# A 64-row pair in place of two 128-row matmuls for the sums that a recurrence adds to later nodes

## The chip, the cores and the metric

The kernel runs on one core of one Trainium2 chip. The metric is the device time of one launch, in microseconds (us): the median over several runs. A profile is one further execution, recorded by the hardware profiler. Five engines matter here: TensorE (PE in the profile; its weight loads are listed apart as PEld), VectorE (DVE), ScalarE (ACT), GpSimd (POOL) and SyncE (SP), which issues most DMAs.

## The reference

Four graph layers follow one another on 16 graphs (B = 16) of 1024 nodes (N) with 256 features (D), all in float32. Each layer is `x = x + layer(relu(layernorm(x)))`, with one adjacency matrix per graph. Layers 0, 1 and 3 are sums over neighbours and dense products. Layer 2, which the change is in, is a recurrence over the nodes:

```
def step(h, i):                                  # for every node i, in order
    x_par = adjT_normalised[:, i] @ h            # sum over the neighbours, by their newest state
    r, z  = sigmoid(split(x[i] @ W_ioux.T + b + x_par @ W_iouh.T + b))
    hc    = tanh(x[i] @ W_coux.T + b + (x_par * r) @ W_couh.T + b)
    h[i]  = z * x_par + (1 - z) * hc
```

Node i needs the new states of earlier nodes and the old states of later ones. The adjacency has about 3% of its entries set.

## The kernel before

**Blocks and sub-blocks.** Layer 2 (`layer_2`, L542) takes the nodes in NT = 8 blocks of P = 128, and each block in NS = 8 sub-blocks of S = 16 nodes. Inside a block the nodes are put in an order of their own, made earlier, so that few nodes of a sub-block depend on each other. The 16 graphs are taken together: a tile holds G2 = 2 groups of GB = 8 graphs, and the 128 partitions of a group are 8 graphs x 16 nodes, the graph the slower index. So the state `h` of a sub-block is [128 rows (graph, node), 2 groups, 256 features].

**One sub-block** is K rounds (`round_`, L807; K is 1 for sub-blocks 0 to 4, then 2, 2 and 4; KS) and, where the graphs call for it, more rounds under a condition. A round is 8 matmuls into `pr` and 8 into `pz`, sigmoids on ACT, products on DVE, 8 matmuls into `pc`, a tanh on ACT, and per group two DVE instructions that give the new `h` (L844, L845). Between two rounds stands `change` (L792).

**What a finished sub-block owes to later nodes** is h times adjacency. `Sub.behind` (L703) spreads the adjacency rows into `bd`, [128 rows (graph, node), group, 8 graphs, later nodes]: row (graph b, node i) is zero in the columns of every graph but b. Three kinds of matmuls use it: `near` (L990) for the next 16 nodes, `next_block` (L750, L752) for the first 16 nodes of the next block, and `far_tasks` (L756) for the rest of the block. The rest is far = 96, 80, 64, 48, 32 or 16 nodes after sub-blocks 0 to 5, and none later. For each of 2 groups, 2 halves c of the features and 2 halves of the 8 graphs there is one far task: one matmul with 4 x far columns (L765) into a PSUM tile `pf`, and one DVE addition into `bxt`, the running sums of the block (L768).

**Fillers.** Far tasks are not run where they arise. They go as `behind` into the list `todo` of the following sub-block, mixed evenly (L918 to L920) with `share`: the tasks of `base_tasks` (L576), which build the next block's first sums from the other seven blocks. BASES says how many graphs are taken in a sub-block (1, 1, 2, 2, 2, 2, 2, 4); for each graph there are 7 matmuls of 256 columns (L616), all into one `pf` tile that is held until ACT has read it (L603), and one turning step (L630) into a `pf` tile of its own. In block 7 there is no next block and no share.

`fill(weight)` (L924) issues the first part of the list at the beginning of the sub-block and the rest in steps. With K = 1 there are two steps: a part of 0.357 ahead of the round's matmuls, and all the rest behind the `pc` matmuls. The parts are measured by each task's own cost, 0.0067 * far for a far task. What must be done behind a task's matmul (the addition, the copy) goes into `late` and is issued by `evict` (L788): in `round_` once behind the `pz` matmuls, and once behind the DVE instructions that give the new `h`.

**Order and buffers.** PE, DVE, ACT and POOL run their instructions in the order in which the program issues them (`manual_schedule`, L869). PSUM has 8 banks: `pr`, `pz`, `pc`, `pnx` and one `pa` take five, and `pf` has the other three (`bufs=3`). Far tasks, base tasks, turning steps and the input products of the next sub-block (`Gates`, L737 and L729) all take their tiles from these three. A fourth tile is written when the first one's reader is through.

Of the kernel before, what the change touches and what calls it, by code (L numbers as in the profile page):

```python
# [9 lines left out]
F32 = mybir.dt.float32  # L10
# [6 lines left out]
P = 128  # L17
B, N, D, H = 16, 1024, 256, 1024
NT = N // P
DC = D // P  # L20
HC = H // P
S = 16
NS = P // S
G2 = 2
GB = B // G2
# [14 lines left out]
def gnn_stack(ctx: ExitStack, tc: tile.TileContext, a: dict, out: bass.AP):  # L40
    nc = tc.nc
# [500 lines left out]
    def layer_2(shared, early):  # L542
        with ExitStack() as st:
            wp = st.enter_context(tc.tile_pool(name="w2", bufs=1))
            psum = st.enter_context(tc.tile_pool(name="psum2", bufs=1, space=PSUM))
# [202 lines left out]
            def next_block(h, bd, n, start):  # L748

                for c in range(DC):  # L750
                    for g in range(G2):
                        nc.tensor.matmul(pnx[:, c, g * GR : (g + 1) * GR], h[:, g, c * P : (c + 1) * P],  # L752
                                         bd[:, g, :, n : n + S], start=start and c == 0 and g == 0, stop=True,
                                         skip_group_check=True)

            def far_tasks(bxt, h, sub):  # L756


                bd, s = sub.bd, sub.s
                far = P - (s + 2) * S  # L760

                def task(g, c, b4):
                    def run():
                        pf = psum.tile([P, 4, far], F32, name="pf", bufs=3)
                        nc.tensor.matmul(pf, h[:, g, c * P : (c + 1) * P], bd[:, g, b4 : b4 + 4, S : S + far],  # L765
                                         start=True, stop=True)
                        to = bxt[:, c, g * GB + b4 : g * GB + b4 + 4, P - far :]
                        return lambda: nc.vector.tensor_add(to, to, pf)  # L768
                    return 0.0067 * far, run
                tasks = []  # L770
                if far > 0:
                    tasks = [task(g, c, b4) for g in range(G2) for c in range(DC) for b4 in (0, 4)]
                if sub.n > P - s * S:
                    tasks.append((0.9, lambda: next_block(h, bd, P - (s + 1) * S, s == 0)))
                return tasks
# [7 lines left out]
            def add(to, lhsT, rhs):  # L783
                nc.tensor.matmul(to, lhsT, rhs, start=False, stop=True, skip_group_check=True)
# [84 lines left out]
            with tc.manual_schedule(engines={mybir.EngineType.PE, mybir.EngineType.DVE, mybir.EngineType.Activation, mybir.EngineType.Pool}):  # L869
# [3 lines left out]
                bxt = shared.tile([P, DC, B, P], F32, name="bxt")  # L873
# [13 lines left out]
                for t in range(NT):  # L887
# [10 lines left out]
                    for s in range(NS):  # L898
# [36 lines left out]
                        for c in range(DC):  # L935
                            to = x[:, c].rearrange("p (b i) -> p b i", b=B)
# [10 lines left out]
                        h = work.tile([P, G2, D], F32, name="h")  # L947
# [38 lines left out]
                        if s + 1 < NS:  # L986
                            near = psum.tile([P, DC, G2 * GR], F32, name="pa")
                            for c in range(DC):
                                for g in range(G2):
                                    nc.tensor.matmul(near[:, c, g * GR : (g + 1) * GR], h[:, g, c * P : (c + 1) * P],  # L990
                                                     sub.bd[:, g, :, :S], start=True, stop=True)
                            behind = far_tasks(bxt, h, sub)
                        elif t + 1 < NT:
                            next_block(h, sub.bd, 0, False)
                            near = pnx
                            behind = last_tasks(t + 1, bxt_next)
                            bxt, he = bxt_next, he_next
# [221 lines left out]
```

## Time and profile before

| | |
|---|---|
| median of 7 runs | 4944.09 us (4938.64 to 4954.79) |
| profiled execution, device time | 4950.51 us |
| its span, first to last instruction | 4948.8 us, granted TensorE clock 0.979 |
| PE busy | 4621.6 us (93%) |
| DVE busy | 2386.8 us (48%) |
| far matmuls (L765), two passes each | 768 passes, 220.7 us busy |
| far additions (L768) | 384, 209 to 555 ns each |

The recurrence lies between about 1450 and 3500 us of the span; far tasks run from 1589.5 to 3428.5 us. A float32 matmul appears in the profile as two passes, each with a weight load (PEld) of its own, so 384 far matmuls are 768 rows. "Mean ns of one" is from a pass's start to its modelled end, longer than the distance to the next pass, because passes overlap: the distance between starts is what a pass takes of PE. In the timeline a row's first two numbers are the start of a group of equal instructions and the time from there to the end of its last one.

### The profile page before, as it was taken

To read this page: it belongs to the slowest core of one execution; us is meant where nothing else is said; L and a number is where in the kernel's file an instruction comes from. 1 tells how busy PE (TensorE), PEld (TensorE's weight loads), DVE (VectorE), ACT (ScalarE), POOL (GpSimd) and SP (SyncE) were. 2 spreads that over 40 slices of the span, in tenths; PEclk is the share of its full clock that TensorE was granted. 3 is DMA by queue.
4 is the path that set the end of the run, shared out by engine and by line. 5 is a ranking of instruction groups with operands and counts; after the bars stand their busy time and mean duration, and the time that the engine had idled before them with its cause. 6 is when DMAs were issued, how large, how long until landed. Compare 5 with 4: busy or idle time off the path is not lost. (4 is left out here: it accounts for less than half of the span.)

```text
span 4948.8 us, 52564 instructions
## 1 busy us (share of the span) xinstructions
PE 4621.6 (93%) x18431; PEld 3061.8 (62%) x18431; DVE 2386.8 (48%) x6366; ACT 1174.6 (24%) x2388; POOL 1599.1 (32%) x1883
## 2 busy tenths in 40 slices
PE   8898899999997999999999999998799999999999
PEld 4443455565555777777777777776365555555656
DVE  6667754446443454445454545455534434334343
ACT  1111112112111222222222222222222323223232
POOL 3122333334323323233222222332523424234232
PEclk9999999999998999999999999999899999999999
DMA  4432335454536444544343434431422222222200
GB/s 157 120 94 94 95 94 179 165 170 151 181 118 191 130 143 121 162 140 149 116 143 106 152 121 158 128 127 34 149 85 85 77 77 85 77 95 69 83 26 17
DMA packets 530500, 577.13 MB, mean 117 GB/s; under 512 B 41552, under 2 KB 438992, under 8 KB 527824
## 3 DMA queue, kind: packets, MB, share of 16 engines
q1 hardware_dynamic: 499056, 460.79, 29.6%
q0 software_dynamic: 31040, 111.44, 6.4%
q8 instruction: 195, 3.19, 0.3%
q14 instruction: 209, 1.71, 0.1%
HBM read 470.17 MB, written 116.65 MB: 119 GB/s over the span
## 5 line engine op out<-in xcount | busy, mean ns | idle before, releaser
L290 PE MATMUL pa<-at,h 128*128 128x512 f32 x1088 | 489.3, 602 | 29.4 <-DVE ag L295 29.4
L1094 PE MATMUL ph<-ag,w 128*128 128x512 f32 x1024 | 479.4, 611 | 33.9 <-DVE hh L1098 33.8
L1132 PE MATMUL po<-w,hh 128*128 128x256 f32 x2048 | 447.7, 379 | 0.0
L616 PE MATMUL pf<-hb,ab 128*128 128x256 f32 x1568 | 422.6, 389 | 22.1 <-ACT bs L603 18.8
L1132 PEld LDWEIGHTS po<-w,hh 128*128 128x128 f32 x2048 | 387.8, 190 | 59.3 <-issue 7.9
L290 PE MATMUL pa<-at,q 128*128 128x512 f32 x960 | 420.8, 594 | 0.0
L290 PEld LDWEIGHTS pa<-at,h 128*128 128x128 f32 x1088 | 207.1, 193 | 269.5 <-issue 227.3
L1094 PEld LDWEIGHTS ph<-ag,w 128*128 128x128 f32 x1024 | 179.1, 190 | 295.9 <-DVE hh L1098 152.2
L1100 POOL TENSOR_TENSOR ss<-ss,sq 128x512 f32<-128x512 f32 x224 | 302.8, 1352 | 121.7 <-ACT sq L1097 117.4
L616 PEld LDWEIGHTS pf<-hb,ab 128*128 128x128 f32 x1568 | 286.4, 195 | 75.2 <-ACT bs L603 26.0
L983 POOL DMA_INDIRECT hs_d<-h,table x128 | 129.9, 1015 | 624.4 <-DVE gz L739 448.9
L290 PEld LDWEIGHTS pa<-at,q 128*128 128x128 f32 x960 | 179.5, 190 | 223.9 <-issue 220.9
L737 PE MATMUL pf<-wx,hs 128*128 128x512 f32 x512 | 243.5, 617 | 29.7 <-POOL hs L720 18.4
L1098 DVE TENSOR_SCALAR hh<-ph,b 128x512 f32<-128x512 f32 x256 | 190.0, 747 | 154.7 <-ACT sq L1097 120.6
L1079 PE MATMUL pa<-bxt,h 128*128 128x512 f32 x512 | 228.1, 598 | 20.1 <-POOL bxt L1061 20.1
L765 PE MATMUL pf<-bd,h 128*128 128x384 f32 (+5 forms) x768 | 220.7, 376 | 27.1 <-DVE bxt L768 27.1
L827 DVE TENSOR_TENSOR r<-r,x 128x256 f32<-128x256 f32 x230 | 124.4, 563 | 228.0 <-ACT r L826 222.9
L1079 PE MATMUL pa<-at,h 128*128 128x512 f32 x512 | 228.8, 597 | 0.0
L1097 ACT ACTIVATE sq<-ph,b 128x512 f32<-128x512 f32 x224 | 153.4, 685 | 234.6 <-PE ph L1094 189.5
L1124 ACT ACTIVATE hh<-hh,rw 128x512 f32<-128x512 f32 x256 | 168.5, 712 | 138.7 <-DVE hh L1123 136.7
L1135 DVE TENSOR_TENSOR x<-x,po 128x256 f32<-128x256 f32 x120 | 50.4, 420 | 289.0 <-PE po L1132 288.9
L1079 PEld LDWEIGHTS pa<-bxt,h 128*128 128x128 f32 x512 | 97.5, 192 | 137.3 <-issue 115.2
(233 smaller groups left out, 7945.8 us busy)
## 6 DMA issues: line engine op xcount, KB each, us to landing
at<-in_adjT SPq DMA_DIRECT2D x64, 1024.0 KB
ab<-in_adj SPq DMA_DIRECT2D x128, 512.0 KB
bxt<-in_adjT SPq DMA_DIRECT2D x64, 512.0 KB
at<-in_adjT SPq DMA_DIRECT2D x64, 512.0 KB
ad<-in_adj SPq DMA_DIRECT2D x128, 128.0 KB
x_d<-x POOLq DMA_DIRECT2D x16, 1024.0 KB
he_d<-h POOLq DMA_DIRECT2D x16, 1024.0 KB, 9.3
heT_d<-hT POOLq DMA_DIRECT2D x16, 1024.0 KB
```

Source lines behind the costliest of these rows:

```text
L290: nc.tensor.matmul(pa, h[:, mt, c * P : (c + 1) * P], at[n0 // 512][:, mt], start=mt == 0, stop=mt == NT - 1)
L616: nc.tensor.matmul(pb, ab[:, jts[k]], hb[:, jts[k]], start=k == 0, stop=k == len(jts) - 1)
L737: nc.tensor.matmul(pg, self.hs[:, c, g * GR : (g + 1) * GR], wx[:, c, D:], start=c == 0, stop=c == DC - 1)
L765: nc.tensor.matmul(pf, h[:, g, c * P : (c + 1) * P], bd[:, g, b4 : b4 + 4, S : S + far], start=True, stop=True)
L983: nc.gpsimd.indirect_dma_start(out=hs_d[t][g][:, :], out_offset=row(1, g, t, s), in_=h[:, g], in_offset=None)
L1079: nc.tensor.matmul(pa, h[b][:, mt, c * P : (c + 1) * P], at[b][n0 // NH][:, mt], start=mt == 0, stop=mt == NT - 1)
L1094: nc.tensor.matmul(ph, w1[:, c, k * P : (k + 1) * P], ag[:, c, n0 : n0 + NH], start=c == 0, stop=c == DC - 1)
L1097: nc.scalar.activation(sq, ph, AF.Square, bias=b1[:, k : k + 1])
L1098: nc.vector.tensor_scalar(hh[:, k], ph, b1[:, k : k + 1], None, op0=ALU.add)
L1100: nc.gpsimd.tensor_tensor(ss, ss, sq, ALU.add)
L1124: nc.scalar.activation(hh[:, k], hh[:, k], AF.Silu, scale=rw[:, k : k + 1])
L1132: nc.tensor.matmul(po, hh[:, c, k * P : (k + 1) * P], w2[:, c], start=c == 0, stop=c == HC - 1)
```

## The change

A far task now does both halves of the graphs at once. The two matmuls that it replaces each took all 128 rows of `h` and of `bd` and the columns of 4 graphs. The new ones take only the 64 rows of those same 4 graphs, rows 0 to 63 for graphs 0 to 3 of the group and rows 64 to 127 for graphs 4 to 7. The rows left out held zeros in these columns. Each writes a `pf` tile of its own, and both additions are made in one closure behind them. The number of matmuls, their columns and the additions are what they were; there are half as many tasks, each with the cost figure of one old task.

```diff
-                def task(g, c, b4):
+                def task(g, c):
+
                     def run():
-                        pf = psum.tile([P, 4, far], F32, name="pf", bufs=3)
-                        nc.tensor.matmul(pf, h[:, g, c * P : (c + 1) * P], bd[:, g, b4 : b4 + 4, S : S + far],
-                                         start=True, stop=True)
-                        to = bxt[:, c, g * GB + b4 : g * GB + b4 + 4, P - far :]
-                        return lambda: nc.vector.tensor_add(to, to, pf)
+                        halves = [psum.tile([P, GB // 2, far], F32, name="pf", bufs=3) for _ in range(2)]
+                        for k, pf in enumerate(halves):
+                            own_rows = slice(k * P // 2, (k + 1) * P // 2)
+                            nc.tensor.matmul(pf, h[own_rows, g, c * P : (c + 1) * P],
+                                             bd[own_rows, g, k * GB // 2 : (k + 1) * GB // 2, S : S + far], start=True, stop=True)
+
+                        def add():
+                            for k, pf in enumerate(halves):
+                                b0 = g * GB + k * GB // 2
+                                to = bxt[:, c, b0 : b0 + GB // 2, P - far :]
+                                nc.vector.tensor_add(to, to, pf)
+                        return add
                     return 0.0067 * far, run
                 tasks = []
                 if far > 0:
-                    tasks = [task(g, c, b4) for g in range(G2) for c in range(DC) for b4 in (0, 4)]
+                    tasks = [task(g, c) for g in range(G2) for c in range(DC)]
```

## The prediction

> **What bounds the kernel now.** I read the page first, then the windows over the recurrence, the far tasks' own rows, and the order of time. The page's busy line and the windows (span, PE, PEld, DVE, ACT, POOL, clock, DMA share, GB/s):
>
> ```profile
> PE 4621.6 (93%) x18431; PEld 3061.8 (62%) x18431; DVE 2386.8 (48%) x6366; ACT 1174.6 (24%) x2388; POOL 1599.1 (32%) x1883
> 1590.00:3306.00 1716.00, 1623.02 (x7989) 1312.90 (x7988) 814.20 (x1934) 433.30 (x1014) 513.91 (x736) 0.98 0.43 136
> 3306.00:3430.00 124.00, 109.02 (x516) 83.33 (x514) 70.99 (x153) 30.45 (x71) 46.93 (x64) 0.99 0.11 36
> ```
>
> PE is busy 95% of blocks 0 to 6 (1623 of 1716 us); DVE under half. So there PE time saved or lost counts in full, and a wait of PE counts as much as a matmul. Block 7, without fillers, has 15 us of idle PE.
>
> The source view of the far line says what it has now:
>
> ```profile
> L765 PE MATMUL pf<-bd,h x768: 219/379/847, 1589.6 to 3428.5; 128*128 128x384 f32 x32, 128*128 128x320 f32 x32, 128*128 128x256 f32 x32, 128*128 128x192 f32 x32
>   DVE bxt L768: 73.2, 100
> ```
>
> 768 passes against 384 additions: two passes to a matmul. 73 us of PE waits already end at the additions, for lack of a free `pf`.
>
> The trace shows no 64-row matmul. Its nearest relative is L342, whose matmuls use 32 of the array's columns, four strips in turn. The timeline around 54.9, 394.5 and 397.6 us:
>
> ```profile
> 54.92 1.05 PE L342 MATMUL pd<-at,gs 128*32 128x512 f32 x2
> 394.25 0.38 PE L391 MATMUL pmm<-w,ag 128*128 128x256 f32 x1
> 394.56 1.06 PE L342 MATMUL pd<-at,gs 128*32 128x512 f32 x8
> 397.16 1.03 PE L342 MATMUL pd<-at,gs 128*32 128x512 f32 x6
> 398.13 1.13 PE L290 MATMUL pa<-at,q 128*128 128x512 f32 x2
> ```
>
> Two things are read here. One matmul (2 passes) takes 1.05 us; four on four strips (8 passes) take 1.06: different strips run side by side. And changing shape costs. L391's pass takes 0.22 us, but L342 begins 0.31 after it: 0.09 late. On the way back, L342's last pass ends at 398.19 and is 0.59 long (592 ns, the median of L342's passes), so it began at 397.60; at 0.43 from start to start, as for all 512-column passes, L290 was due at 398.03 and begins at 398.13, 0.10 late. L290's first two passes then take 1.13 where 0.59 + 0.43 = 1.02 is usual: the first weight load of 128 columns stands in the open, 0.11. So a change of shape with 128-column weights costs 0.10 + 0.11, about 0.20 us; a far pair between base tasks needs two, 0.40.
>
> The order of time in a sub-block with far = 96 shows the buffers, first PE, then DVE:
>
> ```profile
> 2584.23 0.81 PE L765 MATMUL pf<-bd,h 128*128 128x384 f32 x2
> 2584.87 0.59 PE L616 MATMUL pf<-hb,ab 128*128 128x256 f32 x2
> 2585.30 0.81 PE L765 MATMUL pf<-bd,h 128*128 128x384 f32 x2
> 2585.95 0.59 PE L616 MATMUL pf<-hb,ab 128*128 128x256 f32 x2
> 2587.10 0.91 PE L765 MATMUL pf<-bd,h 128*128 128x384 f32 x2 [0.56 <-DVE bxt L768]
> ...
> 2586.16 0.42 DVE L845 TENSOR_TENSOR h<-z,w 128x256 f32<-128x256 f32 x1
> 2586.50 1.01 DVE L768 TENSOR_TENSOR bxt<-bxt,pf 128x384 f32<-128x384 f32 x2
> ```
>
> One `pf` is held by the base sums, two far tasks take the others, and the third waits for an addition that stands on DVE behind the new `h`.
>
> **The matmuls.** Distances between starts give a far matmul 0.64, 0.54, 0.43, 0.32, 0.22 and 0.22 us for 384 to 64 columns (a 64-column one is 0.17 itself, but the next task runs 0.05 longer). A pair is two of these today. After, if halves run side by side as strips do, it is one, plus 0.40:
>
> 384: 1.28 to 1.04; 320: 1.08 to 0.94; 256: 0.86 to 0.83; 192: 0.64 to 0.72; 128 and 64: 0.44 to 0.62.
>
> Four pairs of each per block: side by side saves 4 x 2.37 = 9.5 us, and 24 pairs x 0.40 = 9.6 us of shape changes take it back. The matmuls alone: nothing.
>
> **The buffers.** A pair wants two of three `pf` while the base sums hold one. Its first half goes when one is free, its second one addition later, and a turning step in its wake waits for its addition. Take far = 96, times from the first far task (2573.82). First part of the list now: 3 far, 3 base steps, 3.25 us. After: halved far cost makes it pair, 2 base, pair, turn. Pair 1 ends at 1.04, base at 1.9. DVE adds x and copies the seed until 1.46, then adds pair 1, to 2.0 and 2.5. So pair 2's halves stream from 2.15 and 2.65, and the turn waits for its first addition, to 3.65; the part ends at 4.1, 0.85 later. Second part, from the end of `pc` (2584.23): now 7.1 us (Gates begin at 2591.33). After: base, pair 3, base to 1.9; `h` is ready at 2.35, the additions of pair 3 free their tiles at 2.9 and 3.4, so pair 4 streams from 3.05 and 3.55 and ends at 4.4; three base steps and `next_block` (0.89) bring 6.6, 0.5 earlier, with two pairs in place of five tasks. Net +0.3.
>
> The same steps with 16 base steps (far = 80, 64, 48) give first part 5.06, 4.65, 4.5 for 4.38, 4.21, 4.03, and second part 9.44, 9.0, 8.74 for 10.14, 9.64, 9.16 (today's 11.84, 11.34, 10.86 less 1.7 at half clock, below): net 0, -0.2, -0.1. With far = 32 and 16 the pairs lose 4 x 0.18 = 0.7 and, from the rows' DVE times (0.28, 0.21 an addition), some 0.5 and 0.2 of new waits: +1.2 and +0.9. A block: 0.3 + 0 - 0.2 - 0.1 + 1.2 + 0.9 = +2.1; seven blocks +15 us. The bounds: no wait beyond today's leaves the matmuls' 0; every one of 168 pairs waiting out two additions (0.55, 0.48, 0.41, 0.35, 0.28, 0.21, mean 0.38) gives 168 x 0.76 = +128. I take the worked sub-blocks, since they are this code's own order.
>
> Block 7: pairs follow each other in two runs with K = 1, so shape changes halve; the first part shortens by 0.9 (far = 96: 1.94 to 1.04), the second gains 0.6 behind the wait for `h`. I count 0.
>
> **The clock.** PE stalls carry a second price. At 2613.0 to 2616.2, after waits of 0.94 and 0.78 us, the windows give a granted clock of 0.50, and two base passes take 0.83 instead of 0.43. About 3.4 us at half speed loses 1.7; 0.98 over the 1716 us is some 34 us lost already. The new waits in far = 96 (1.05 and 0.5) come near those that set it off. Five more windows: +9 us; between 10 fewer (-17) and 15 more (+25).
>
> Untouched: DVE's work (384 additions of the same shapes), the DMAs and their queues.
>
> **The sum.** 0 + 15 + 9 = +24 us, on the profiled 4950.5 (span 4948.8, 1.7 around it): 4974.5; the profiled execution is 6.4 above the median 4944.1, so 4968 on the median.
>
> Two rules of the Trainium skill bear on this. "TensorE: Matmul & The Clock Gate", Part 3, has matmuls start and end strictly in program order; by that, the second pass of the first half would hold back the second half, a pair would be three passes, and the sum 5006; L342's 8 passes in 1.06 us, two per matmul, speak against it. "TensorEngine Tiling (Array Packing)", Tiling Modes, lists 64 x 128 as a mode and says that a change of mode drains TensorE; that speaks against this change and for the 0.40, which the trace shows for column strips only.
>
> **The rivals.**
> Faster: a change between 128 rows and 64 rows is cheap, because both use all 128 columns and nothing drains. For it: L342 changes the columns, and only that is shown. Against: the open weight load is one of 128 columns. At no cost the sum is -66 (7 x 9.5) + 15 + 9 - 5 (block 7) = -47: 4897; at 0.10 a change, 168 x 0.20 = 34 come back: 4931. It decides below 0.28 us a round trip, (66 + 5 - 24) / 168.
> Slower by more: the halves do not run side by side. Then the 9.5 us saved are missing in 8 blocks: 24 + 76 = +100, 5044; half of it (three passes for four) 5006. For it: no 64-row pass is shown; against: the strips.
> No change: the additions hide behind base tasks and the clock is not touched: 0 to +8, 4944 to 4952. For it: today's third task waits too, in the same place. Against: a pair's second half waits for one addition more.
>
> **How the numbers follow.** Forecast 0.50 (its own range 4953 to 4992: waits of 9 to 24 and clock 0 to 25), halves one behind the other 0.14, no change 0.11, cheap changes 0.25. This kernel's measurement can tell about 0.2%, 10 us, from no change. Of the forecast 0.02 falls below that bound: faster 0.25, same 0.13, slower 0.62. The range drops the far ends of the cheap-change case (below 4905) and of the serial case (above 5020), some 0.2 together.
>
> **What would show it.** Right: L765 rows with 64 rows, the two halves of a pair starting within some 0.02 us of each other where both buffers are free, a gap of 0.1 ahead of a pair and one behind it; PE waits that end at L768 up from 73 us; base passes behind a pair with a longer first pass; more stretches at clock 0.50. Wrong: no gap at the shape change (the cheap case), a second half that starts 0.3 us or more behind the first without a wait (the serial case), or waits at L768 no longer than today's.

## The result and the profile after

After takes 4976.97 us (median of 17 runs, 4964.90 to 4983.74), before 4949.69 (42 runs on the same chips, 4933.00 to 4966.79): +27.3 us, ratio 1.0057 [1.0049, 1.0066]. The profiled executions agree: span 4977.4 for 4948.8, granted clock 0.975 for 0.979. Of the 28.6 us between the spans 25.0 lie between the first far task and the start of the last sub-block, and 5.0 in that last sub-block, which has no far task but 20.5 us at half clock where before had 10.2.

The page's busy line, and the windows over the recurrence (span, PE, PEld, DVE, ACT, POOL, clock, DMA share, GB/s) up to block 7 and in block 7:

```profile
PE 4645.6 (93%) x18431; PEld 3012.8 (61%) x18431; DVE 2376.4 (48%) x6366; ACT 1175.5 (24%) x2388; POOL 1601.5 (32%) x1883
```

```profile
1588.00:3327.00 1739.00, 1635.53 (x7990) 1264.50 (x7989) 803.82 (x1934) 433.91 (x1015) 514.49 (x736) 0.98 0.43 135
3327.00:3451.00 124.00, 110.12 (x502) 77.29 (x501) 70.69 (x148) 28.74 (x67) 46.92 (x64) 0.94 0.11 36
```

Blocks 0 to 6 go from 1716 to 1739 us with the same instructions. PE's busy time rises with the span (1623 to 1636): a pass at half clock counts as busy for longer (0.83 us for 0.43 in before), and so does a pass whose weight load stands in the open. DVE's does not rise (814 to 804). Block 7 runs at a clock of 0.94 where before had 0.99.

The source view of the far line, matmuls and weight loads together:

```profile
L768 PEld LDWEIGHTS pf<-bd,h x768: 182/186/335, 1588.0 to 3453.4; 64*128 64x128 f32 x192
L768 PE MATMUL pf<-bd,h x768: 272/427/1006, 1588.0 to 3453.5; 64*128 64x384 f32 x32, 64*128 64x320 f32 x32, 64*128 64x256 f32 x32, 64*128 64x192 f32 x32
...
  DVE bxt L775: 69.5, 106
  issue: 25.6, 78
```

The passes now have 64 rows. The idle time that ends at the additions is 69.5 us, where before had 73.2; new is the idle time put down to "issue", 78 times 0.33 us; all of it stands before weight loads, which are not made ahead at a shape change (with pairs on 128 rows, below, it comes 6 times). The waits of PE's matmuls alone (total, times, longest) show which ones grew:

```profile
PE pf L616 <- ACT bs L603: 26.6, 18, 1.5
PE pf L768 <- DVE bxt L775: 23.5, 44, 1.7
PE pf L630 <- DVE bxt L775: 13.8, 37, 0.6
```

In before these were 18.8, 27.1 (L765) and 1.5. The far matmuls wait no longer than they did. The base sums (L616) wait longer for the tile that the copy `bs` reads, and the turning step (L630) now finds its tile held by a far sum 37 times, where it did 5 times. All three are waits for a `pf` tile; together 47.4 became 63.9.

PE's timeline in block 5, sub-block with far = 96, and a closer window around its first pair:

```profile
2853.52 0.92 PE L768 MATMUL pf<-bd,h 64*128 64x384 f32 x4
2854.37 1.13 PE L616 MATMUL pf<-hb,ab 128*128 128x256 f32 x4
2855.50 1.37 PE L768 MATMUL pf<-bd,h 64*128 64x384 f32 x4
2857.05 0.71 PE L630 MATMUL pf<-to,bs 128*128 128x128 f32 x4 [0.18 <-DVE bxt L775]
...
2863.93 0.59 PE L616 MATMUL pf<-hb,ab 128*128 128x256 f32 x2
2864.46 0.92 PE L768 MATMUL pf<-bd,h 64*128 64x384 f32 x4
2865.30 0.70 PE L616 MATMUL pf<-hb,ab 128*128 128x256 f32 x2
2866.81 1.37 PE L768 MATMUL pf<-bd,h 64*128 64x384 f32 x4 [0.81 <-DVE bxt L775]
```

```profile
2853.21 0.39 PE L998 MATMUL pa<-bd,h 128*128 128x128 f32 x2
2853.52 0.59 PE L768 MATMUL pf<-bd,h 64*128 64x384 f32 x2
```

The closer window holds two passes of the pair, one of each half, in 0.59 us: side by side. All four take 0.92 where both tiles are free, and 1.37 where the second half waits for its tile, which is 0.45 lost inside the pair that no wait in brackets shows. Of 192 pairs 115 start their halves together (6 to 7 ns apart); in most of the others the second half starts 0.15 to 0.46 us late, in five pairs of block 7 0.57 to 2.15 us.

In the sub-block with far = 32 of block 4 the longest wait of before ahead of a far task or turning step is 0.33 us. After has these, ahead of a pair and ahead of a turning step:

```profile
2718.87 0.68 PE L768 MATMUL pf<-bd,h 64*128 64x128 f32 x4 [0.53 <-DVE bxt L775]
2721.87 0.49 PE L768 MATMUL pf<-bd,h 64*128 64x128 f32 x4
2722.99 0.71 PE L630 MATMUL pf<-to,bs 128*128 128x128 f32 x4 [0.63 <-DVE bxt L775]
```

### The profile page after: what moved, and what is told of

The parts are those of the page before. It is cut to its first block, busy times and chain, and to the rows that moved or that the text cites. A ratio compares the mean times of both kernels' runs of the same rounds, so it can differ in the third digit from the quotient of the medians.

```text
span 4977.4 us, 52554 instructions
## 1 busy us (share of the span) xinstructions
PE 4645.6 (93%) x18431; PEld 3012.8 (61%) x18431; DVE 2376.4 (48%) x6366; ACT 1175.5 (24%) x2388; POOL 1601.5 (32%) x1883
## 3 DMA queue, kind: packets, MB, share of 16 engines
q1 hardware_dynamic: 499056, 460.79, 29.4%
## 5 line engine op out<-in xcount | busy, mean ns | idle before, releaser
L616 PE MATMUL pf<-hb,ab 128*128 128x256 f32 x1568 | 422.5, 396 | 31.2 <-ACT bs L603 26.6
L616 PEld LDWEIGHTS pf<-hb,ab 128*128 128x128 f32 x1568 | 278.9, 194 | 101.9 <-issue 37.6
L739 DVE TENSOR_TENSOR gz<-pf,bzc 128x512 f32<-128x512 f32 x128 | 87.4, 690 | 214.7 <-PE pf L737 214.1
L834 ACT ACTIVATE r<-pr 128x256 f32<-128x256 f32 x230 | 75.7, 381 | 456.0 <-PE pr L792 372.3
```

Source lines behind the costliest of these rows:

```text
L616: nc.tensor.matmul(pb, ab[:, jts[k]], hb[:, jts[k]], start=k == 0, stop=k == len(jts) - 1)
```

## The experiments

My theory at first: the time comes from two tiles wanted at once; the row halves as such cost as much as they save, and lone row halves would lose. The rivals: the row halves themselves cost the time, or the place of the pairs in the list of fillers does.

Two numbers go with each kernel below. **Tile waits** are the PE waits for a `pf` tile in the rows shown above (L616, L630 and the far line, those that end at an addition, or at `bs` for L616 and the far line). **Half clock** is the time, from the first far task to the start of the last sub-block, that the trace's clock records give at 0.50; it comes in stretches of some 3.4 us, and half of it is lost. Both are of one profiled execution each. "Corrected" is a change of the recurrence's blocks 0 to 6, from the start of each sub-block to the next, with half of the half-clock time taken off; where exactly a sub-block is taken to start moves such a figure by about 1 us. "At full clock" is an estimate from every execution on record: its span times its granted clock, averaged over a kernel's executions, less the same of before on that chip.

| kernel | us against before, same chip | ratio | tile waits | half clock |
|---|---|---|---|---|
| before | | 1 | 47.4 | 61.4 |
| after | +27.3 | 1.0057 [1.0049, 1.0066] | 63.9 | 85.3 |
| cost of a pair doubled | +30.5 | 1.0067 [1.0051, 1.0082] | 55.3 | 75.1 |
| pairs on 128 rows | +4.0 | 1.0012 [1.0001, 1.0022] | 60.2 | 37.5 |
| lone matmuls on 64 rows | +122.6 | 1.0254 [1.0227, 1.0280] | 35.5 | 160.4 |
| pairs for far = 96, 80 only | -0.9 | 1.0001 [0.9991, 1.0012] | 50.9 | 75.1 |
| after, h first | -14.5 | 0.9973 [0.9963, 0.9982] | 57.6 | 30.7 |
| before, h first | -51.3 | 0.9900 [0.9885, 0.9915] | 22.0 | 30.7 |
| pairs on 128 rows, h first | -29.4 | 0.9943 [0.9927, 0.9959] | 48.6 | 13.7 |
| wide | -55.1 | 0.9892 [0.9873, 0.9910] | 33.6 | 30.7 |
| wide, h first | -93.4 | 0.9813 [0.9800, 0.9826] | 7.2 | 30.7 |

(Of the 55.3 with the cost doubled, 6.0 stand ahead of far matmuls and end at the turning step's copy, L631. Lone matmuls were run twice, the others 4 to 17 times.)

**The place in the list.** The cost figure of a pair is that of one old task; doubled, the pairs spread over the list as two tasks did.

```diff
-                    return 0.0067 * far, run
+                    return 2 * 0.0067 * far, run
```

> The changed kernel with the cost figure of a pair doubled, so that it weighs as much in the mix as the two tasks it replaces. My theory (shape changes eat what side-by-side halves save; the rest is waits for pf tiles and half-clock stretches): the two parts of a list differ by one base step only, so the time stays near the changed kernel, 20 to 32 us above the kernel before. Rival (the halved cost figure pushes the far work forward and that is what costs the time): back to the kernel before, within 6 us of it.

4979.73 us against 4949.21: the same loss as after. The cost figure is not the cause.

**Pairs on 128 rows.** The pair stays, with its two tiles at once; each matmul takes all rows again, so no halves run side by side and no shape changes.

```diff
-                            nc.tensor.matmul(pf, h[own_rows, g, c * P : (c + 1) * P],
-                                             bd[own_rows, g, k * GB // 2 : (k + 1) * GB // 2, S : S + far], start=True, stop=True)
+                            nc.tensor.matmul(pf, h[:, g, c * P : (c + 1) * P],
+                                             bd[:, g, k * GB // 2 : (k + 1) * GB // 2, S : S + far], start=True, stop=True)
```

> The changed kernel with both matmuls of a pair on all 128 rows: the pairs, their two tiles and the closure with two additions stay, the row halves go. My theory: the matmuls alone are worth nothing either way (9.5 us a block saved by side by side, 9.6 lost by shape changes), so this runs 10 to 32 us above the kernel before, within 12 us of the changed kernel; far = 96 and 80 get dearer, far = 32 and 16 cheaper. Rival 1 (the row halves cost the time, the pairing is harmless): within 6 us of the kernel before. Rival 2 (the row halves save and the pairing costs more than that): over 35 us above the kernel before.

4953.19, a loss of 4 us only. By the raw time the row halves cost 23 of the 27 us, which is what the rival said. But the same two windows read:

```profile
1588.00:3309.00 1721.00, 1617.94 (x7987) 1299.23 (x7985) 808.24 (x1933) 433.40 (x1014) 515.08 (x736) 0.99 0.43 136
3309.00:3433.00 124.00, 111.53 (x520) 84.44 (x520) 72.01 (x155) 30.77 (x71) 47.12 (x64) 0.99 0.11 36
```

The clock is higher than in after, in block 7 0.99 for 0.94: 37.5 us at half clock for after's 85.3. Half of the difference, 24 us, is the difference of the two times. Corrected, this kernel is 15.8 us over before and after is 15.9: at equal clock, row halves and full rows cost the same. That does not hang on one profile: at full clock, before comes to 4840 us (23 executions on this chip), this kernel to 4856 (12) and after to 4856 (19). Its waits are nearly after's, fewer at the turning step alone:

```profile
PE pf L616 <- ACT bs L603: 26.6, 18, 1.5
PE pf L768 <- DVE bxt L775: 23.6, 46, 1.5
PE pf L630 <- DVE bxt L775: 10.0, 20, 0.6
```

So the pairing, two tiles at once and two additions behind each other, costs some 16 us with either kind of rows, and the row halves come with more half-clock time. My expectation of the time failed, because I had put the clock down to the waits. That far = 96 and 80 would get dearer and 32 and 16 cheaper failed too: per block, corrected, the sub-blocks from far = 96 down to 16 cost -0.39, +0.33, +0.26, +0.28, +1.57 and +0.63 us here, within 0.2 us of after's, listed further below.

**Lone matmuls on 64 rows.** Before's tasks one by one, each on its own 64 rows: a shape change each, nothing beside it, one tile at a time.

```diff
-                        nc.tensor.matmul(pf, h[:, g, c * P : (c + 1) * P], bd[:, g, b4 : b4 + 4, S : S + far],
+                        own_rows = slice(b4 * S, (b4 + 4) * S)
+                        nc.tensor.matmul(pf, h[own_rows, g, c * P : (c + 1) * P], bd[own_rows, g, b4 : b4 + 4, S : S + far],
```

> The kernel before with each far matmul on its own 64 rows, one task each as before, so that every far task stands alone between 128-row matmuls. My theory: 336 lone tasks in blocks 0 to 6 pay two shape changes of 0.20 us each, 134 us, less what falls into waits that are there already (62 us of them in these blocks): 80 to 140 us above the kernel before. Rival (64 rows next to 128 rows cost nothing): within 15 us of it.

5071.84 against 4949.21. The source view of its far line:

```profile
L766 PE MATMUL pf<-bd,h x768: 272/427/1007, 1589.4 to 3552.2; 64*128 64x384 f32 x32, 64*128 64x320 f32 x32, 64*128 64x256 f32 x32, 64*128 64x192 f32 x32
...
  issue: 82.2, 241
```

241 idle times of 0.34 us with no releaser, where after has 78 and the pairs on 128 rows have 6. It has fewer tile waits than before (35.5) and is the slowest kernel here: the shape change is dear, it is paid per task, and 99 us more at half clock come with it. Corrected it loses 75.5 us, the clock the rest; by two executions it is +83 at full clock, 0.22 us a lone matmul.

**Pairs for large far only.** For far = 96 and 80 after's task, here named `pair`; below that before's tasks.

```diff
-                if far > 0:
-                    tasks = [task(g, c) for g in range(G2) for c in range(DC)]
+                if far >= 80:
+                    tasks = [pair(g, c) for g in range(G2) for c in range(DC)]
+                elif far > 0:
+                    tasks = [task(g, c, b4) for g in range(G2) for c in range(DC) for b4 in (0, 4)]
```

> Pairs on row halves for far = 96 and 80 only, single 128-row tasks as before for far = 64 to 16. My theory: the two traces give -0.55 us a block for far = 96 and +0.3 for far = 80, so blocks 0 to 6 come out 2 us below the kernel before, and half-clock stretches move it by up to 10 either way: -10 to +8. Rival (waits for the additions cost the time, and they are longest for far = 96 and 80): 15 us or more above the kernel before.

4948.30: no change, as expected, with 3.5 us more tile waits than before and 14 us more at half clock. The loss of after sits in the pairs with far = 64 and less.

**What holds the tiles: h first.** In the sub-blocks with far = 80, 64 and 48 I found `h` late, in before too. ACT's timeline there, before:

```profile
2606.35 0.59 ACT L833 ACTIVATE w<-pz 128x512 f32<-128x512 f32 x1
2608.98 0.47 ACT L603 ACTIVATE bs<-pf,dinv 128x256 f32<-128x256 f32 x1 [2.04 <-PE pf L616]
2609.36 0.65 ACT L843 ACTIVATE hc<-pc 128x256 f32<-128x256 f32 x2
```

`pc` was through at 2607.38. The tanh on it (L843) runs at 2609.36, behind a copy `bs` that `fill` issued ahead of it and that waits for the base sums, matmuls issued behind `pc`. In after it is the same. Far additions stand behind `h` on DVE, so a late `h` holds far tiles. The next two kernels issue the second part of the list behind the instructions that give `h`, in after and in before.

```diff
-                fill()
                 hc = work.tile([P, G2, D], F32, name="hc", bufs=1)
                 for g in range(G2):
                     nc.scalar.activation(hc[:, g], pc[:, g], AF.Tanh)
                     nc.vector.tensor_mul(w[:, g], w[:, g], hc[:, g])
                     nc.vector.tensor_add(to[:, g], z[:, g], w[:, g])
+                fill()
```

> The changed kernel with the filler call of a round's end moved behind the tanh and the products that give the new h: PE's order is the same, but the fillers' instructions on ACT and DVE (the copy of the base sums, the additions) no longer stand ahead of or among these. My theory (in sub-blocks 2 to 4 the tanh stands on ACT behind the copy bs, which waits for base matmuls, so h is late, the additions stand behind h, and PE waits for their pf tiles): the PE waits that end at bs (26.6 us) and at the additions (37 us) fall by half or more, and the stretches at half clock (85 us inside the recurrence) with them: 20 to 50 us under the changed kernel, 25 under to 8 over the kernel before. Rival (the waits belong to the three tiles and the additions' own time, whatever h does): within 8 us of the changed kernel, 20 or more above the kernel before.

> The same move in the kernel before. My theory: its waits have the same root (18.8 us end at bs, 27.1 and 1.5 at the additions, 61 us at half clock): 20 to 55 us under the kernel before, and e5 comes within 10 us of it, because without the waits the row halves are worth what the matmuls alone say, nothing. Rival (waits by tiles and additions): within 8 us of the kernel before.

4932.12 and 4895.29 against 4946.60. ACT in the same sub-block of before with `h` first:

```profile
2575.18 0.59 ACT L833 ACTIVATE w<-pz 128x512 f32<-128x512 f32 x1
2576.47 0.66 ACT L842 ACTIVATE hc<-pc 128x256 f32<-128x256 f32 x2 [0.70 <-PE pc L784]
2577.82 0.84 ACT L603 ACTIVATE bs<-pf,dinv 128x256 f32<-128x256 f32 x2 [0.68 <-PE pf L616]
```

Here the tanh follows the end of `pc` (2576.21) by 0.26 us, before by 1.98. The move is worth 51 us to before. Of the 54 between the profiled spans 39 are left when corrected and 15 are the clock's; the 39 sit in the sub-blocks with far = 80, 64 and 48 (1.3 to 1.5 us each in a block) and in the last sub-block of a block (1.1). I had expected the pairs' cost to go with it; instead it grew, from 27 to 37 us, at the same half clock (30.7 in both). In after the waits at `bs` fell as expected (26.6 to 5.6), but those at the additions, which were to halve, rose from 37 to 52. First the waits of before, then those of after, both with `h` first:

```profile
PE pf L765 <- DVE bxt L768: 12.2, 25, 1.5
PE pf L616 <- ACT bs L603: 8.9, 18, 0.6
...
PE pf L630 <- DVE bxt L768: 0.9, 4, 0.3
```

```profile
PE pf L630 <- DVE bxt L775: 20.9, 41, 0.6
PE pf L768 <- DVE bxt L775: 18.4, 25, 1.7
PE pf L616 <- DVE bxt L775: 12.7, 12, 1.1
PE pf L616 <- ACT bs L603: 5.6, 6, 0.9
```

22.0 us became 57.6, +35.6, and the corrected time says +37.5 (+32 at full clock). In before the base sums never waited for a far addition; with pairs and `h` first they do, 12 times. So a late `h` had covered part of what the pairs cost.

**Full rows again, h first.** The pairs on 128 rows with the same move, to part tiles from rows a second time.

> Pairs with both matmuls on all 128 rows, and the filler call behind the new h: e5 without the row halves, e6 with the pairing. e5 runs 37 us above e6 with the same time at half clock, and its PE waits that end at the additions are 52 us against 13. My theory now (two tiles at a time of three are what costs; the row halves net nothing): this is within 10 us of e5, 27 to 47 us above e6. Rival (the shape changes cost, once the waits that covered them are gone): within 10 us of e6.

4919.36 against 4948.78. By the differences to the kernel before it is 21.9 above before with the move and 14.9 below after with it. Corrected, two tiles at once cost 28.7 us (tile waits +26.6), the row halves another 8.9 (tile waits +9.0, most of it at the turning step, 13.4 to 20.9) and 17 us more at half clock. At full clock it is 23 for the tiles and 8 for the row halves. The result lies between the two theories: the tiles are the larger part, the row halves the smaller.

**Wide: fewer tiles.** If tiles are what is short, before with fewer of them should gain. For far of 64 and less the columns of all 8 graphs fit one tile; one matmul and one addition do what two did.

```diff
...
+                def wide(g, c):
+                    def run():
+                        pf = psum.tile([P, GB, far], F32, name="pf", bufs=3)
+                        nc.tensor.matmul(pf, h[:, g, c * P : (c + 1) * P], bd[:, g, :, S : S + far], start=True, stop=True)
+                        to = bxt[:, c, g * GB : (g + 1) * GB, P - far :]
+                        return lambda: nc.vector.tensor_add(to, to, pf)
+                    return 2 * 0.0067 * far, run
...
```

> The kernel before with one matmul over all 8 graphs of a group and one addition, where 8 x far columns fit a tile (far = 64 to 16): half the matmuls, tiles and additions there. My theory: the matmuls win 4 x 0.22 us a block for far = 16 and nothing else (7 us in 8 blocks), and with half as many tiles PE waits less for them in sub-blocks 3 to 6: 5 to 20 us under the kernel before. Rival (an addition of 512 elements holds its tile longer, so the waits stay): 0 to 8 us under it.

4891.48 against 4946.60, -55 us, much more than expected. Tile waits fall by 13.8 and half clock by 30.7 (15 us); corrected, the sub-blocks with wide tasks gain 17.5 (far = 16), 3.4 (32), 7.0 (48) and 6.3 us (64). I did not separate what of this is the matmuls, the weight loads and the waits.

**Both.** `wide` with `h` first.

> Both: one matmul over 8 graphs for far up to 64, and the filler call behind the new h. If the two take the same waits away, this equals e6 within 8 us; if they are separate, it is 5 to 15 us under e6. Both theories have it under the kernel before, by 25 to 60 us if the h order is the root and by 0 to 15 if it is not.

4853.15 against 4946.60, the fastest kernel here and 42 us under before with `h` first, where neither theory had more than 15. The two gains (51 and 55) stand nearly whole beside each other. One wait for an addition is left of any size:

```profile
PE pf L765 <- DVE bxt L768: 4.9, 8, 1.0
...
PE pf L616 <- ACT bs L603: 2.3, 6, 0.4
```

**Row halves on top of it.** In this kernel with nearly no tile waits, the pairs on 64 rows, after's `task`, for far = 96 and 80 (first), and for far = 64 and 48 a task of four matmuls, both feature halves on both row halves in two tiles (second), with half the additions of before and as many as `wide`.

```diff
                 if far > 64:
-                    tasks = [task(g, c, b4) for g in range(G2) for c in range(DC) for b4 in (0, 4)]
+                    tasks = [task(g, c) for g in range(G2) for c in range(DC)]
```

```diff
...
+                        halves = [psum.tile([P, DC, GB // 2, far], F32, name="pf", bufs=3) for _ in range(2)]
+                        for c in range(DC):
+                            for k, pf in enumerate(halves):
+                                own_rows = slice(k * P // 2, (k + 1) * P // 2)
+                                nc.tensor.matmul(pf[:, c], h[own_rows, g, c * P : (c + 1) * P],
+                                                 bd[own_rows, g, k * GB // 2 : (k + 1) * GB // 2, S : S + far], start=True, stop=True)
...
```

> e9 with row-half pairs for far = 96 and 80, where they save 0.24 and 0.14 us a pair. My theory (the pairs' tiles give it back): e9 within 8 us, -8 to +8. Rival (with h early the tiles come free in time and the saving stays): 8 to 12 us under e9.

> e9 with, for far = 64 and 48, one task of four row-half matmuls for a group: both feature halves of 4 graphs in one tile, two tiles, two additions, and two shape changes for four matmuls. By the measured passes a group takes 1.26 and 1.04 us in place of 1.72 and 1.28: 1.4 us a block less PE, 11 us in 8 blocks. If PE time decides: 5 to 12 us under e9. If two tiles at a time decide here as well: 0 to 20 us above e9, with the PE waits that end at the additions up by as much.

4860.14 and 4856.16 against 4948.78: ratios 0.9824 [0.9807, 0.9842] and 0.9815 [0.9798, 0.9832], where the kernel under them has 0.9813. Here the row halves change nothing that can be told. Tile waits go from 7.2 to 19.2 and 16.9 us. The half-clock time of the profiled executions falls from 30.7 to 17.1 and 6.8, but over all executions the granted clock is no different (0.981 to 0.984 in these two, 0.981 to 0.983 under them). At full clock the three are 77 (under them), 69 and 78 us under before: the first loses some 8 us to its tiles, the second nothing. The 5 to 12 us that the passes alone would have saved in the second do not show.

**The shape change alone.** Why do the row halves come with more half-clock time? Pairs on 128 rows, and behind each pair one matmul of 64 rows and 2 columns into unused columns of its second tile: the shape changes as often as in after, nothing runs on half rows for long.

```diff
+                        nc.tensor.matmul(tiles[1][:, 510:], h[: P // 2, g, c * P : (c + 1) * P], bd[: P // 2, g, 0, S : S + 2],
+                                         start=True, stop=True)
```

> e2 (pairs on all 128 rows, 37.5 us at half clock inside the recurrence in its profile) with one more matmul behind each pair, of 64 rows and 2 columns, into two unused columns: the change of shape and back without row-half streaming. By the passes measured in the changed kernel it costs 0.10 + 0.11 + 0.11 + 0.10 + 0.11 = 0.53 us where a pair stands alone, 89 us for 168 pairs, less what falls into waits: 50 to 95 us above e2 at equal clock. What is open is why the changed kernel has 85 us at half clock and e2 37.5. If the gaps at the shape changes set it off: 75 us or more here. If passes on half of the rows do: under 55 us here.

5009.97 against 4944.11, ratio 1.0127 [1.0106, 1.0148]. 192 shape changes forth and back cost 62 us over the pairs on 128 rows (+65.9 for +4.0), 0.32 us a round trip with its tiny matmul and the clock in it; at full clock it is 47, just under the 50 to 95 expected, while tile waits fall from 60.2 to 40.0. Half clock is 61.4 us, between those of the pairs on 128 rows (37.5) and of after (85.3). That alone is no answer to the question.

The traces together say more. Cut each of the 14 from the first far task to the last into pieces of 3.41 us, the length of the shortest clock records, and add up for each piece how long its passes stream at full clock (0.43 us for 512 columns, 0.32 for 384, 0.21 for 256), with a pass of 64 rows counted half. Of the 161 pieces at full clock where the sum is under 0.38 of the piece, 144 are followed by a piece at 0.50; of the 7103 others, 7 are. With 64-row passes counted whole, 41 of those 151 drops have a sum of 0.38 or more in place of 7. So by these traces the clock falls after a piece in which the array was given too little to do, and a pass on half of the rows counts for half: gaps, waits and half rows all add to it. This is a count over finished traces; no kernel was made to test it.

## Why the prediction was right, point by point

**Predicted +24 us, measured +27.3; slower, as forecast.** The largest part of the sum, the wait for tiles, is confirmed, and in its size: +15 predicted, +15.9 corrected. Of the profiled +28.6 the rest is 12.0 from half clock in the same stretch, 5.0 in the last sub-block, -2.6 in block 7 (corrected) and some -2 elsewhere.

**The matmuls: nothing.** Right in the sum. The halves start 6 to 7 ns apart; the gap ahead of a pair is 0.097 us and the weight load behind it stands in the open for 0.107. A pair of 384 columns takes 0.845 from its first start to the next instruction, 0.64 for its passes, 0.107 for its own first weight load in the open and 0.10 for the gap behind it. So the round trip of 0.40 taken from column strips holds for row halves too: 0.097 + 0.845 + 0.107 is 1.05, where 1.04 was predicted. The pairs on 128 rows have the same corrected time, 15.8 and 15.9. But the saving and the shape changes do not show by size: the passes alone give a block -0.96 us for far = 96 and +0.72 for 16, and after less the pairs on 128 rows is within 0.2 us for both. What is shown is that neither reaches the time while PE waits for tiles. With `h` first the row halves lost 8.9, so the nothing is good to some 10 us. The rule of strict program order that the prediction weighed ("TensorE: Matmul & The Clock Gate", Part 3) holds for the matmuls as wholes but does not describe their passes: the second half's first pass starts with the first half's first pass, ahead of the first half's second; where the second half waits for its tile, it comes behind it.

**The buffers: +15.** Right in the sum, less so in its parts. (The parts worked for far = 48, +0.47 and -0.42, make +0.05 and not -0.1; the seven blocks are then +16.) The order of time for far = 96 came out nearly as worked: the second pair starts 1.98 us behind the first for 2.15, the turning step 3.53 for 3.65, and the fourth pair 2.88 behind the end of `pc` for 3.05. Per block, predicted and measured: far = 96 +0.3 and -0.38; 80 0 and +0.20; 64 -0.2 and +0.13; 48 -0.1 and +0.45; 32 +1.2 and +1.74; 16 +0.9 and +0.57; the sub-blocks without far tasks, which I had left out, -0.44. That the loss sits in far = 32 and 16 was the prediction's, and is what the kernel with pairs for 96 and 80 alone shows.

**Where the waits would be.** Wrong in a detail: L768's waits did not rise above 73. That number counted weight loads with the matmuls (46 of 73.2 us); the matmuls' own waits were 27.1 and became 23.5. The rise came at the next in line for a tile, the turning step (+12.3) and the base sums (+7.8). The prediction's working had the turn waiting in far = 96; its list of signs named the wrong line.

**Block 7: 0.** From its first far task to the start of its last sub-block 122.7 us became 125.2, with 13.7 us at half clock for 3.4: corrected -2.6. The clock had no term for block 7, nor for the last sub-block (+5.0).

**The clock: +9.** 24 us more at half speed, 12 us: the size came near by luck, since the reason given does not hold. I had tied it to the new waits, but the pairs on 128 rows have nearly the same waits and less half-clock time than before. It goes with the half-row passes in three pairs of kernels (+48, +17 and +99 us), and not by chance of one execution: the granted clock is 0.974 to 0.979 in 19 executions of after and 0.978 to 0.982 in 12 of the pairs on 128 rows. In the two kernels on top of the wide one, with fewer half-row passes, it did not rise. By the count over all traces, half-row passes and gaps leave more pieces under 0.38; that no kernel tested.

**The rivals.** Cheap shape changes are ruled out by the passes: 0.41 us a round trip, where that rival needed less than 0.28. (The lone matmuls' +122.6 has some 40 us of clock in it.) Halves one behind the other are ruled out by the closer window. No change is ruled out by the interval.

## What to carry to other kernels

A tile that holds a result until a slower engine has read it is a resource like an engine: before two matmuls are made to run together, count the tiles that they hold at once and ask who stands behind them. A PE wait says which line waits, not who is to blame; compare the sum of all waits for the same pool of tiles. And look for a copy in an in-order queue ahead of the critical instruction: moving it was worth 51 us here, and fewer, wider tasks 55, where matmuls side by side gave nothing.

## What the runs showed of the hardware that was not expected

Two passes of different row halves start 6 to 7 ns apart when both tiles are free; when the second tile is not, both passes of the first half can run ahead of the second's.

Narrower rows save nothing alone: 384 lone matmuls of 64 rows cost 122.6 us more than those of 128 rows, 0.32 us each, of it 0.22 at full clock.

Half-clock stretches of some 3.4 us stand amid dense work: in before one followed waits of 0.94 and 0.78 us. The Trainium skill ("TensorE: Matmul & The Clock Gate", Part 1) has the clock fall after an idle window of about 3.4 us; no such idle window preceded that one: in the 3.41 us ahead of it passes streamed for 0.38 of the time. Their total, 6.8 to 160.4 us between kernels of the same work, moves the time as much as the edits do, so a difference of a few per thousand is read only beside the clock.
